# Where six splits of x are issued: in front of the first gate/up pair, or inside it

## The chip, the cores and the metric

The kernel runs on one core of one Trainium2 chip. The metric is device time in microseconds (us): the median of several executions of the same program.

## The reference

One transformer block on x of 2048 rows and 1024 columns, all in float32:

```python
x = x + layernorm(attn(layernorm(x)))       # one head, d = 256, over all 2048 keys
x = x + layernorm(ffn(layernorm(x)))
# attn: qkv = x @ Wqkv + bqkv; softmax(q k^T / 16) v; @ Wo + bo
# ffn:  (silu(x @ W_gate.T) * (x @ W_up.T)) @ W_down.T   with 2752 hidden features
```

## The kernel before

**Precision.** Every float32 operand of a matmul is split in two: `hi`, a cast to fp32r on ScalarE, and `lo`, the rest, by a subtraction on VectorE. A product is then three matmuls, hi·hi, hi·lo and lo·hi. Such pairs of instructions come from `split` (lines 108 and 109) and, where their order is pinned, from `split_later` (lines 406 and 407).

**Attention** runs over 16 blocks of 128 queries. For block i there are `turn` (transposes of the probabilities), `scores` of the next block, `attend` (lines 275 and 276, which read v from the tile `a1` and the transposed probabilities from `a2`), `turn_o` (transposes of the output, line 284, then a split into `oTs`) and `proj` (the matmuls of lines 145 to 147 against `wo_s`, which lies in the tile `wvo`; line 294 adds the bias `bo_s` and scales). `turn_o` and `proj` of block i are issued in step i + 1, those of the last block, NT - 1, after the loop.

**The feed-forward part** works on two halves of 1024 rows. A half has ten pairs of feature blocks (`gate_up`), a rest, and the down projection (`run_down`). A pair is a Strassen-like product of 2 x 2 blocks: seven products, each for gate and for up, each of 12 matmuls (line 604), whose x operands are B11, B21, T2, T1, T3, T4 and B22 in this order. B11 and B21 are parts of x; the T are sums and differences of parts. Four PSUM banks (ag, au, cg, cu; bank 0 to bank 3 in the first half) hold the results. The products with T2 go on accumulating in ag and au, so the first results must be copied out of these banks before: lines 636 and 638. After each group VectorE adds (line 617) and ScalarE applies silu (line 620).

**Where x comes from.** The split operands of the first half lie in `xb` (B11, B21), `kx` (T1, T3), `qa` and `qb` (T2) and `a1` (T4, B22). `a1` is v's tile during attention, and `kx`, `qa`, `qb` hold k and q. The sums of x (line 383) are made during attention and parked in DRAM (`xs_d`). Ten objects of the class `First` bring them back: `load` issues two DMAs (line 428) into a staging tile, `use` splits it into its place (lines 406 and 407). Their list is

```python
order = [t2[0], t13[0], t13[1], t13[2], t2[1], t13[3]] + t4
```

The first four use the staging tiles `f4[2]`, `f4[3]`, `wr[1]` and `xe`, and are split inside the last step of attention. The other six use the same four tiles again; numbers 4 and 5 are the second half of T2 (into `qb`) and the last part of T1/T3 (into `kx`), numbers 6 to 9 are T4 and B22 (into `a1`).

**What sets the order.** A scheduler of the language orders the instructions of each engine by a timeline of its own, from the order of the trace and the dependencies; pinned instructions keep their order in the program among themselves. All these loads and stores go through SP's queue: among them the attention outputs `at_d` (line 296), gate/up weights (line 510, into `f4[4]`, `f2p` and `wr[0]`) and down-projection weights (line 728, into `f4[0:2]`). The weights are split by `Pair.prep` into slots of `a2` and `wvo` as these come free.

**Background jobs.** `gate_up` calls `background()` at three places, which pops one job each. In the first half the jobs of pair p are `ahead(p)` (transposes and loads of late rows, line 346 and 957/958, and sums of down weights, line 733) and `behind(p)` (loads of down weights, the residual of a late row, lines 301 to 307). The staging tiles `wr[1]` and `bo_s` later go to a ring, `raws2`, for the second half and the end.

Of the kernel before, what the change touches and what calls it, by code (L numbers as in the profile page):

```python
# [34 lines left out]
def block_kernel(ctx, tc, x, wqk, wv, bqk, bv, wo, bo, wgu, wlast, wd, out):  # L35
# [17 lines left out]
    def tl(p, shape, dt, name):  # L53
        return p.tile(shape, dt, tag=name, name=name, bufs=1)
# [7 lines left out]
    bo_s = tl(cpool, [P, C], F32, "bo_s")  # L62
# [30 lines left out]
    f4 = [tl(cpool, [P, C], F32, f"f4_{i}") for i in range(5)]  # L93
# [187 lines left out]
    def turn_o(i):  # L281
        b = bank[5][:, 0:D]
        for d in range(2):
            nc.tensor.transpose(b[:, d * P : (d + 1) * P], o_s[i % 2][:, d * P : (d + 1) * P], ident)
        split(oTs[i % 2][:, :, 0, :], oTs[i % 2][:, :, 1, :], b.rearrange("p (d q) -> p d q", d=2))

    def proj(i):
        a = pair[i % 3][0] if i < EARLY else f4[i % 2]
        oT = oTs[i % 2]
        for h, b in ((1, bank[5]), (0, bank[7])):  # L290
            cols = slice(h * 512, h * 512 + 512)
            for d in range(2):
                mm3(b, (oT[:, d, 0, :], oT[:, d, 1, :]), (wo_s[:, d, 0, cols], wo_s[:, d, 1, cols]), d == 0, d == 1)
            nc.vector.scalar_tensor_tensor(a[:, cols], b, ys[i % 4][:, 13:14], bo_s[:, cols], ALU.mult, ALU.add)
        if i >= EARLY:
            nc.sync.dma_start(at_d[i], a)
# [23 lines left out]
    wr = [tl(wpool, [P, C], F32, f"wr{i}") for i in range(2)]  # L320
# [20 lines left out]
    def xpose(t, a, b, banks):  # L341
        for hf in range(2):
            o = banks[hf]
            for j in range(4):
                cb = 4 * hf + j
                nc.tensor.transpose(o[:, j * P : (j + 1) * P], a[:, cb * P : (cb + 1) * P], ident)  # L346
            s = b[:, hf * 512 : hf * 512 + 512]
            nc.scalar.copy(s, o)  # L348
            d = xT_d[t // TB][hf * 512 : hf * 512 + 512, (t % TB) * P : (t % TB + 1) * P]
            nc.sync.dma_start(d.rearrange("(j p) t -> p j t", p=P), s.rearrange("p (j t) -> p j t", j=4))  # L350
# [18 lines left out]
    def xq(name, cb):  # L369
        if name == "T2":  # L370
            return q2[cb // 2][:, cb % 2, :, :]
        t, c = XQ[name]
        return t[:, c + cb, :, :]
# [79 lines left out]
    raws2 = Ring([])  # L453
# [33 lines left out]
    def w4(t):  # L487
        return t.rearrange("p (c h f) -> p c h f", h=2, f=P)
# [112 lines left out]
    def mmc(o, w, m, first, last, chained, pin=lambda m: m):  # L601

        for n, (i, j) in enumerate(((0, 0), (0, 1), (1, 0))):
            one = nc.tensor.matmul(o, w[i], m[j], start=first and n == 0, stop=last and n == 2, skip_group_check=chained)  # L604
            if n == 0:
                pin(one)

    def prod(o, w, a, b, first=True):

        slot, c0 = w.at[a]  # L610
        v = w4(slot.need())
        for cb in range(4):
            x = xq(b, cb)
            mmc(o, (v[:, c0 + cb, 0, :], v[:, c0 + cb, 1, :]), (x[:, 0, :], x[:, 1, :]), first and cb == 0, cb == 3, not first)

    def add(o, a, b, op=ALU.add):
        nc.vector.tensor_tensor(o, a, b, op)  # L617

    def silu(o, a):
        nc.scalar.activation(o, a, AF.Silu)  # L620

    def gate_up(s, p, wg, wu, bg, jobs):

        ag, au, cg, cu = bg
        g11, g12, g22, g21, u11, u12, u22 = tmp[0:7]
        job = list(jobs)

        def background():
            if job:
                job.pop(0)()  # L630

        def put(name, t):
            nc.sync.dma_start(hd[s][p][name], t)

        prod(ag, wg, "A11", "B11")
        nc.scalar.copy(g11, ag)
        prod(au, wu, "A11", "B11")
        nc.scalar.copy(u11, au)
        prod(cg, wg, "A12", "B21")
        wg.slot[0].done()  # L640
        add(g11, cg, g11)
        silu(g11, g11)
        prod(cu, wu, "A12", "B21")
        wu.slot[0].done()
        add(u11, cu, u11)
        add(g11, g11, u11, ALU.mult)
        put("A11", g11)
        background()
        prod(ag, wg, "S2", "T2", False)
        nc.scalar.copy(g12, ag)  # L650
        prod(au, wu, "S2", "T2", False)
        nc.scalar.copy(u12, au)
        prod(cg, wg, "S1", "T1")
        wg.slot[1].done()
        prod(cu, wu, "S1", "T1")
        wu.slot[1].done()
        background()
        prod(ag, wg, "S3", "T3", False)
        nc.scalar.copy(g22, ag)
        add(g22, cg, g22)  # L660
        silu(g22, g22)
        prod(au, wu, "S3", "T3", False)
        nc.scalar.copy(u22, au)  # L663
        add(u22, cu, u22)
        add(g22, g22, u22, ALU.mult)
        put("A22", g22)
        background()
        prod(ag, wg, "A22", "T4", False)
        wg.slot[3].done()
        silu(g21, ag)  # L670
        prod(au, wu, "A22", "T4", False)
        wu.slot[3].done()
        add(g21, au, g21, ALU.mult)
        put("A12", g21)
        prod(cg, wg, "S4", "B22", False)
        wg.slot[2].done()
        add(g12, cg, g12)
        silu(g12, g12)
        prod(cu, wu, "S4", "B22", False)
        wu.slot[2].done()  # L680
        add(u12, cu, u12)
        add(g12, g12, u12, ALU.mult)
        add(u22, g12, g22)
        add(u12, g11, g12, ALU.subtract)
        add(u11, u22, g11, ALU.subtract)
        add(g12, g21, u11, ALU.subtract)
        put("S1", u22)
        put("S3", u12)
        put("S2", u11)
        put("S4", g12)  # L690
# [35 lines left out]
    def load_down(p):  # L726
        for r, fb in zip(f4[0:2], (p, p + NPAIR)):
            nc.sync.dma_start(r, wd[fb * P : (fb + 1) * P, :])

    def down_weights(p):  # L730

        r1, r2 = f4[0:2]
        pin(nc.vector.tensor_tensor(r2[:, R], r2[:, R], r1[:, R], ALU.subtract))
        add(r1[:, R], r1[:, R], r1[:, L], ALU.subtract)
        add(r1[:, L], r2[:, R], r1[:, L])
        add(r2[:, L], r2[:, L], r1[:, L], ALU.subtract)
        for n, t in (("T1", r1[:, R]), ("T3", r2[:, R]), ("T2", r1[:, L]), ("T4", r2[:, L])):
            nc.sync.dma_start(td[p][n], t)
# [145 lines left out]
    for i in range(NT):  # L884
# [35 lines left out]
        if i == NT - 2:  # L920
# [3 lines left out]
            order = [t2[0], t13[0], t13[1], t13[2], t2[1], t13[3]] + t4  # L924
            spare = f4[2], f4[3], wr[1], xe
            for f, r in zip(order, spare):
                f.load(r)
    for n in range(4, 6):
        order[n].load(spare[n % 4])
        order[n].use()  # L930
    turn_o(NT - 1)
    proj(NT - 1)
    for n in range(6, 10):
        order[n].load(spare[n % 4])
        order[n].use()
    spool.release()
    xipool = pool("xi")
    xi = [tl(xipool, [P, C], F32, f"xi{i}") for i in range(4)]
    y = f4[0:4] + xi
    tmp = [xi[i // 2][:, (i % 2) * 512 : (i % 2) * 512 + 512] for i in range(8)]  # L940
    raws2.free(wr[1])
    raws2.free(bo_s)
    for n in range(2, 4):
        slots.free(flat(a2[:, 2 * n : 2 * n + 2, :, :]))
    for n in range(2):
# [3 lines left out]
    def late(p):  # L949
        return EARLY + p if 0 <= p < NT - EARLY else None  # L950

    def ahead(p):

        if late(p - 1):
            xpose(late(p - 1), *f4[2:4], Y[0:2])
        if late(p):
            nc.sync.dma_start(f4[2], at_d[late(p)])
            nc.sync.dma_start(f4[3], x[late(p) * P : (late(p) + 1) * P, :])
        down_weights(p)

    def behind(p):
        if p + 1 < NPAIR:
            load_down(p + 1)
        if late(p):
            residual(late(p), *f4[2:4])

    load_down(0)
    for s in range(2):
        pairs, rest, dn = half[s]
        bg, other = (X, Y) if s == 0 else (Y, X)  # L970
        for p in range(NPAIR):
            jobs = [] if s else [lambda: ahead(p), lambda: behind(p)]
            gate_up(s, p, *pairs[p], bg, jobs)
        gate_up_rest(s, *rest, bg)

        def next_x(cb):
            r1, r2 = raws2.get(), raws2.get()
            build_x(2, cb, r1, r2)
            raws2.free(r1)
            raws2.free(r2)  # L980

        if s == 0:
            run_down(s, dn, other, bg, 2 * TB * [None], [lambda cb=cb: next_x(cb) for cb in range(4)])
        else:
            xpool.release()
            x1pool = pool("x1", side="right")
            x1 = [tl(x1pool, [P, C], F32, f"x1_{k}") for k in range(2 * TB)]
            run_down(s, dn, other, bg, x1, [lambda k=k: nc.sync.dma_start(x1[k], x1_d[2 * TB + k]) for k in range(2 * TB)])
# [39 lines left out]
```

## Time and profile before

| | |
|---|---|
| median of 3 runs | 1729.71 us (1728.43 to 1729.87) |
| the profiled execution's own time | 1728.61 us |
| its span in the trace | 1726.8 us |
| mean granted TensorE clock | 0.992 |
| TensorE busy (PE) | 1699.3 us, 98% of the span |
| VectorE busy (DVE) | 1091.8 us, 63% |
| ScalarE busy (ACT) | 689.1 us, 40% |
| GpSimd busy (POOL) | 89.0 us, 5% |
| moved by DMA | 271.01 MB, mean 157 GB/s |

PE is TensorE's matmuls and PEld its weight loads, which lie beside them. A line such as L604 is a line of the kernel's source; helpers such as `split` put all their instructions on one line, so the tile names tell them apart (buffer numbers are left out: `a` stands for `a1` and `a2`, `f` for `f4` and `f2`, `bank` for all eight). Times within the trace are from the start of the span. The hand-over from attention to the first pair lies near 440 to 460 us.

### The profile page before, as it was taken

To read this page: it belongs to the slowest core of one execution; us is meant where nothing else is said; L and a number is where in the kernel's file an instruction comes from. 1 tells how busy PE (TensorE), PEld (TensorE's weight loads), DVE (VectorE), ACT (ScalarE), POOL (GpSimd) and SP (SyncE) were. 2 spreads that over 40 slices of the span, in tenths; PEclk is the share of its full clock that TensorE was granted. 3 is DMA by queue.
4 is the path that set the end of the run, shared out by engine and by line. 5 is a ranking of instruction groups with operands and counts; after the bars stand their busy time and mean duration, and the time that the engine had idled before them with its cause. 6 is when DMAs were issued, how large, how long until landed. Compare 5 with 4: busy or idle time off the path is not lost.

```text
span 1726.8 us, 21119 instructions
## 1 busy us (share of the span) xinstructions
PE 1699.3 (98%) x7788; PEld 1393.6 (81%) x7788; DVE 1091.8 (63%) x1666; ACT 689.1 (40%) x1031; POOL 89.0 (5%) x118
## 2 busy tenths in 40 slices
PE   8999999999899999999999999999999999999997
PEld 7888887888688888888888888788888888888886
DVE  8633667667877777676378457866555564345458
ACT  3222445544544444443355444433333333244343
POOL 1000001000011111110000000100000000000001
PEclk8999999999899999999999999999999999999999
DMA  6221023234755566665358655633332223486654
GB/s 210 80 80 37 37 74 125 97 126 172 257 195 195 201 215 214 214 204 190 122 191 255 194 194 193 205 105 113 129 109 94 91 92 122 132 280 195 195 185 159
DMA packets 131015, 271.01 MB, mean 157 GB/s; under 512 B 13280, under 2 KB 29792, under 8 KB 130912
## 3 DMA queue, kind: packets, MB, share of 16 engines
q1 hardware_dynamic: 128176, 262.72, 45.6%
q10 hardware_dynamic: 2736, 6.95, 1.1%
q8 instruction: 61, 1.00, 0.2%
q14 instruction: 42, 0.34, 0.1%
HBM read 185.73 MB, written 83.89 MB: 156 GB/s over the span
## 4 chain that ended last, share of the span: by engine, by line
PE 93%; DVE 3%; DMA 2%; issue 1%; ACT 1%; POOL 0%; SPq 0%; POOLq 0%; DVEq 0%; ACTq 0%
PE bank L604 70%; PE bank L146 4%; PE bank L145 4%; PE bank L147 4%; PE bank L275 3%; PE bank L276 2%; PE bank L267 1%; PE bank L205 1%; PE bank L206 1%; PE bank L346 1%; DMA f<-x 1%; PE bank L138 1%; DVE small L115 0%; PE bank L773 0%; PE bank L774 0%
## 5 line engine op out<-in xcount | busy, mean ns | idle before, releaser
L604 PE MATMUL bank<-a 128*128 128x512 f32 x1176 | 273.8, 390 | 0.0
L604 PEld LDWEIGHTS bank<-a 128*128 128x128 f32 x1176 | 220.8, 188 | 46.8
L604 PE MATMUL bank<-xb,a 128*128 128x512 f32 x816 | 197.3, 395 | 0.0
L109 DVE TENSOR_TENSOR a<-f2p,a 128x1024 fp32r<-128x1024 f32 (+2 forms) x114 | 124.7, 1095 | 93.4 <-ACT a L108 81.0
L617 DVE TENSOR_TENSOR xi<-bank,xi 128x512 f32<-128x512 f32 (+1 forms) x168 | 113.3, 685 | 111.1 <-PE bank L604 70.1
L604 PEld LDWEIGHTS bank<-xb,a 128*128 128x128 f32 x816 | 152.9, 187 | 37.1
L604 PE MATMUL bank<-kx,a 128*128 128x512 f32 x648 | 157.1, 395 | 0.0
L604 PE MATMUL bank<-a,a 128*128 128x512 f32 x648 | 153.4, 390 | 0.0
L108 ACT CAST a<-f2p 128x1024 fp32r<-128x1024 f32 (+2 forms) x114 | 107.6, 949 | 112.5 <-PE bank L604 102.4
L109 DVE TENSOR_TENSOR a<-f,a 128x512 fp32r<-128x512 f32 (+3 forms) x93 | 91.3, 981 | 91.4 <-ACT a L108 88.0
L604 PEld LDWEIGHTS bank<-kx,a 128*128 128x128 f32 x648 | 121.5, 187 | 29.5
L604 PEld LDWEIGHTS bank<-a,a 128*128 128x128 f32 x648 | 121.6, 188 | 26.4
L604 PE MATMUL bank<-wvo 128*128 128x512 f32 x600 | 142.4, 390 | 0.0
L604 PEld LDWEIGHTS bank<-wvo 128*128 128x128 f32 x600 | 112.6, 188 | 24.4
L108 ACT CAST a<-f 128x512 fp32r<-128x512 f32 (+3 forms) x93 | 69.4, 747 | 125.7 <-PE bank L604 90.6
L275 PE MATMUL bank<-a,a 128*128 128x512 f32 x256 | 94.5, 402 | 2.8 <-ACT f L348 2.0
L109 DVE TENSOR_TENSOR wvo<-f2p,wvo 128x1024 fp32r<-128x1024 f32 (+2 forms) x48 | 54.8, 1141 | 66.2 <-ACT wvo L108 57.6
L604 PE MATMUL bank<-a,wvo 128*128 128x512 f32 x384 | 93.7, 396 | 1.2 <-ACT xi L663 1.2
L604 PE MATMUL bank<-kx,wvo 128*128 128x512 f32 x384 | 91.9, 390 | 0.0
L617 DVE TENSOR_TENSOR xi<-xi,xi 128x512 f32<-128x512 f32 x124 | 85.4, 688 | 4.3
L604 PEld LDWEIGHTS bank<-a,wvo 128*128 128x128 f32 x384 | 72.0, 188 | 18.8 <-ACT xi L663 1.6
L604 PEld LDWEIGHTS bank<-kx,wvo 128*128 128x128 f32 x384 | 72.1, 188 | 15.7
(234 smaller groups left out, 2751.2 us busy)
## 6 DMA issues: line engine op xcount, KB each, us to landing
f2p<-wgu SPq DMA_DIRECT2D x43, 512.0 KB, 5.0
hd_S<-xi SPq DMA_DIRECT2D x80, 256.0 KB, 4.6
f<-x SPq DMA_DIRECT2D x30, 512.0 KB, 3.9
hd_A<-xi SPq DMA_DIRECT2D x60, 256.0 KB, 2.0
f<-wgu SPq DMA_DIRECT2D x21, 512.0 KB, 4.4
wr<-wgu SPq DMA_DIRECT2D x20, 512.0 KB, 5.9
f<-wd SPq DMA_DIRECT2D x20, 512.0 KB, 5.0
td_T<-f SPq DMA_DIRECT2D x40, 256.0 KB, 4.5
```

The source lines that it names most:

```text
L108: nc.scalar.copy(hi, src)
L109: (lo_engine or nc.vector).tensor_tensor(lo, src, f32(hi), ALU.subtract)
L138: nc.tensor.transpose(b[:, j * P : (j + 1) * P], t[:, cb * P : (cb + 1) * P], ident)
L145: nc.tensor.matmul(o, w[0], m[0], start=first, stop=False)
L146: nc.tensor.matmul(o, w[0], m[1], start=False, stop=False)
L147: nc.tensor.matmul(o, w[1], m[0], start=False, stop=last)
L205: nc.tensor.matmul(b, xg[:, c, 0, cols], wv_s[:, c, :, :].rearrange("p a f -> p (a f)"), start=(c == 0), stop=False)
L206: nc.tensor.matmul(b[:, D:], xg[:, c, 1, cols], wv_s[:, c, 0, :], start=False, stop=(c == 7))
L275: nc.tensor.matmul(b, p[:, k, 0, :], vt[:, k, :, :].rearrange("p h d -> p (h d)"), start=(k == 0), stop=False)
L276: nc.tensor.matmul(b[:, D:], p[:, k, 1, :], vt[:, k, 0, :], start=False, stop=(k == NKB - 1))
L604: one = nc.tensor.matmul(o, w[i], m[j], start=first and n == 0, stop=last and n == 2, skip_group_check=chained)
L617: nc.vector.tensor_tensor(o, a, b, op)
```

## The change

Six of the ten `First` objects are used elsewhere. The loads of numbers 4 to 7 are traced after the last `proj`, with `bo_s` (the bias tile, done with by then) in the place of `xe`. Numbers 4 and 5 are split in a new job `first`, which runs in pair 0 after the copy of u11 (line 638), at a new, fourth `background()` place; this job also issues the loads of numbers 8 and 9. In the other pairs `first` is empty, and `ahead` and `behind` keep their places. Numbers 6 to 9 are split at the head of `ahead(0)`, after the first group's result is stored. `wr[1]` and `bo_s` go to `raws2` there.

```diff
@@ gate_up
         prod(au, wu, "A11", "B11")
         nc.scalar.copy(u11, au)
+        background()
         prod(cg, wg, "A12", "B21")
@@ after the attention loop
-    for n in range(4, 6):
-        order[n].load(spare[n % 4])
-        order[n].use()
     turn_o(NT - 1)
     proj(NT - 1)
-    for n in range(6, 10):
-        order[n].load(spare[n % 4])
-        order[n].use()
+
+    last = f4[2], f4[3], wr[1], bo_s
+    for n in range(4, 8):
+        order[n].load(last[n % 4])
     spool.release()
...
-    raws2.free(wr[1])
-    raws2.free(bo_s)
...
+    def first(p):
+        if p == 0:
+            for n in range(4, 6):
+                order[n].use()
+                order[n + 4].load(last[n % 4])
+
     def ahead(p):
 
+        if p == 0:
+            for n in range(6, 10):
+                order[n].use()
+            raws2.free(wr[1])
+            raws2.free(bo_s)
         if late(p - 1):
...
-            jobs = [] if s else [lambda: ahead(p), lambda: behind(p)]
+            jobs = [] if s else [lambda: first(p), lambda: ahead(p), lambda: behind(p)]
```

## The prediction

> **What bounds the kernel now.** I read the page first: engine totals, then the chain that ended last.
>
> ```profile
> PE 1699.3 (98%) x7788; PEld 1393.6 (81%) x7788; DVE 1091.8 (63%) x1666; ACT 689.1 (40%) x1031; POOL 89.0 (5%) x118
> ...
> PE 93%; DVE 3%; DMA 2%; issue 1%; ACT 1%; POOL 0%; SPq 0%; POOLq 0%; DVEq 0%; ACTq 0%
> ```
>
> TensorE is busy for 98% of the span and is 93% of the chain. Work moved between other engines is worth only the time in which TensorE stands still or is slowed. So I looked for TensorE's holes. At the hand-over from attention to the first pair, TensorE's timeline (start, length, engine, line, operands; in brackets the idle time before and who ended it) has:
>
> ```profile
> 441.79 0.39 PE L147 MATMUL bank<-wvo,oTs 128*128 128x512 f32 x1
> 442.44 0.44 PE L284 MATMUL bank<-ident,f 128*128 128x128 f32 x2 [0.26 <-DVE f L279]
> 443.82 0.50 PE L145 MATMUL bank<-wvo,oTs 128*128 128x512 f32 x1 [0.94 <-ACT oTs L108]
> ...
> 446.31 0.80 PE L145 MATMUL bank<-wvo,oTs 128*128 128x512 f32 x1 [1.76 <-DVE oTs L109]
> ...
> 450.31 0.63 PE L147 MATMUL bank<-wvo,oTs 128*128 128x512 f32 x1
> 454.29 2.93 PE L604 MATMUL bank<-qa,a 128*128 128x512 f32 x6 [3.35 <-ACT xi L636]
> ```
>
> Idle: 0.26 + 0.94 + 1.76 + 3.35 = 6.3 us. The same stretch in windows (busy time of PE, PEld, DVE, ACT, POOL, then granted clock):
>
> ```profile
> 444.00:445.00 1.00, 0.55 (x2) 0.12 (x2) 1.00 (x3) 1.00 (x2) 0.00 (x0) 1.00 0.99 397
> 446.00:447.00 1.00, 0.69 (x2) 0.60 (x3) 1.00 (x3) 0.17 (x1) 0.00 (x0) 0.50 0.77 184
> 458.00:459.00 1.00, 1.00 (x4) 0.81 (x3) 1.00 (x2) 0.00 (x0) 0.00 (x0) 0.50 0.01 4
> ```
>
> The clock falls to half inside the hole and is back only near 459. Ten projection matmuls from 446.31 take 4.4 us, at 0.43 each; a full-speed one takes 0.23 (24 L604 in 5.60 us, 462.17 to 467.77). Loss 2.1. The first 12 products, 454.29 to 459.38, take 5.1 for 2.8: loss 2.3. The hole costs 6.3 + 2.1 + 2.3 = 10.7 us. Why it lasts, ScalarE shows:
>
> ```profile
> 441.50 1.05 ACT L406 CAST qb<-f 128x1024 fp32r<-128x1024 f32 x1
> 442.45 1.05 ACT L406 CAST kx<-f 128x1024 fp32r<-128x1024 f32 x1
> 443.39 0.37 ACT L108 CAST oTs<-bank 128x256 fp32r<-128x256 f32 x1
> ...
> 452.71 1.04 ACT L406 CAST a<-f 128x1024 fp32r<-128x1024 f32 x1 [0.49 <-DMA f<-xT_d]
> 453.66 0.58 ACT L636 COPY xi<-bank 128x512 f32<-128x512 f32 x1
> ```
>
> The copy of the first product (L636) frees bank 0 for T2's product, and stands behind the last split of T4. The chain of waits in this window says what that split waited for:
>
> ```profile
> 446.74 5.89 DMA f<-xT_d
> ...
> 453.75 0.49 ACT xi L636
> ```
>
> [...]
>
> **The change part by part.** Nothing is added or removed in number: the six late splits (two T2/T3, four T4) stay six casts L406 and six subtractions L407, with 12 loads L428. The built program of the changed kernel gives the new order on each engine; times come from the trace. Repeat distances when back to back: ScalarE 0.95 for a 1024-wide cast, 0.5 for a 512-wide; VectorE 1.14 and 0.60, L294 0.66.
>
> 1. The cast of T4's first block now precedes the 512-wide cast of 440.71. Its loads left at 436.27 and 436.64; similar ones land in 3.2 and 3.5, so 440.2. It ends its turn at 441.15: the output transposes start at 442.85, not 442.44. Bounds: 0 to +1.3 (landing 439.5 to 441.5); I take +0.4.
> 2. The oTs cast is no longer behind qb and kx: ready at about 443.6, nearly as now. Its subtraction on VectorE loses the L407s of 442.96 and 444.69, two times 1.14: it runs at 443.95, not 445.83. The ten projection matmuls start at 444.35, not 446.31, and at 0.23 end at 446.75.
> 3. On ScalarE there then stand the 1024-wide cast into wvo, which waits for projection's reads (446.2), a 512-wide cast, and L636: 446.2 + 0.95 + 0.5 + 0.5 = 448.2. The first T2 product starts at 448.2, not 454.29: **-6.1 us**.
> 4. Clock. Holes are now about 0.9, 0.5, 0.3 and 1.4 us with work between them[...]. I take full speed: another **-2.3**; the 12th product ends at 451.0 against 459.38, so **-8.4**. The trace has no half-busy stretch like it, so both ends are kept: 0 or +2.7 (two slow projections, 0.4, and 12 slow products, 2.3).
> 5. Who waits for the moved splits, done against needed. qb cast 449.6 against 450.0; kx cast 450.6 against 453.6; their subtractions 453.9 and 455.0 against 456.2 and 458.3. T4's subtractions: first two 456.8 and 457.9 against 465.0 and 465.7; last two 464.2 and 465.9 against 466.4 and 469.4. Behind the casts ScalarE queues the table load (1.28) and silu, then the bank copies of T2's products, needed at 459.3. Zero cost: TensorE turns to qa, kx products meanwhile. If that cover goes, each us late is a us.
> 6. SP's queue. The two loads into bo_s replace those into xe and go after projection's last add: 448.0 and 448.8, not 437.4; at the slowest landing seen here for such a load (5.9), 454.7, used by a cast at about that time. The last four leave when qb and kx are split: 454.3 to 455.5, not 444.2 to 446.7, landing by 461.4; their casts have their turn at 460.9 and 461.9. at_d, wgu and wd transfers pass ahead. Zero, up to +1 with a 7 us landing.
> 7. Afterwards. VectorE does six L407s (6.8 us) later relative to TensorE, so its lead shrinks. In before, pair 1's L636 ended at 490.05 for a product at 496.3: 6.2 us spare. With my order it ends near 486.4 for 486.9: 0.5 spare. Next, pair 1's u11 copy (L638) stands behind a weight cast released by TensorE itself, 0.95, and the copy of the transposed row, 0.5, so TensorE waits: **+1.0**; plus 0.2 for the thin margin. Bounds 0 to +3.
>
> From pair 2 on the order is the old one and TensorE was without holes, so nothing returns. Sum: -8.4 + 1.0 + 0.2 = **-7.2 us**. Against the profiled execution (1728.61, span 1726.8) that is 1721.4; that execution is 1.1 below the median, 1729.71, so the median forecast is 1722.5.
>
> **The rivals.**
> - Half clock stays. Against it: no hole over 1.5 us. For it: the windows show the drop with some work inside. -7.2 + 2.7 = -4.5: 1725.2.
> - VectorE becomes the bound in pairs 0 and 1. For it: busy 0.96 and 0.94 of the windows 450 to 460 and 470 to 480, and a spare of 0.5. If it is 3.5 us later than worked out, -3.7: 1726.0.
> - Slower: T4's last loads. They leave about 9 us later, wait for two splits, and hold ScalarE's in-order queue, behind which stands the bank 0 copy for T4's product (needed at 464.8). Past about 462, each us goes to TensorE. The gain is gone at 469; it's 0.2% slower from 473, 18 us after issue. The slowest landing listed in this stretch is 7.2 (f<-x), against it. Price at 475: +5.8, 1735.5.
> - The change doesn't do what it says, because the scheduler puts the splits back: 1729.7. The built order speaks against it: qb's and kx's casts follow both bank copies.
>
> **How the numbers follow.** Main case 0.62 (1720.9 to 1725.2 by the bounds of steps 1 and 7), half clock 0.20, VectorE late 0.12, late loads 0.05, no effect 0.01. A measurement tells 0.2%, 3.5 us, from no change. Faster: 0.62 + most of half clock, 0.15, + a little of the third, 0.03 = 0.80. Same 0.15. Slower 0.05. Range 1720.0 to 1726.5: from just below the main case's lower end, since steps are rounded to tenths, to just past the VectorE case.
>
> **What would show it.** Right: L604 on qa starting near 448, with the hole under 3.5 us in all, 0.23 per matmul in it, oTs' subtraction before 444.5, L636 ahead of qb's cast; a TensorE wait of about 1 us on L638 near 493. Wrong: granted clock 0.5 after 446 (first rival); PE waiting for L407, L617 or L636 of pair 1 for several us (second); PE idle until a cast after a landing past 462 (third).

## The result and the profile after

| | median us | against the kernel before, same chip |
|---|---|---|
| before | 1728.41 (1726.91 to 1729.87, 14 runs) | |
| changed | 1725.49 (1722.46 to 1729.04, 14 runs) | 0.9981 [0.9974, 0.9989] |

By this ratio the changed kernel is faster by 0.19%, 3.3 us [1.9, 4.5]; the two medians are 2.9 apart. The forecast was a gain of 7.2 (from 1729.71 to 1722.5), so less than half of it came. The profiled execution of the changed kernel took 1725.89, its span is 1724.1.

The page of the changed kernel: engine totals (busy us, share, instructions) and the shares of the chain that ended last:

```profile
PE 1696.0 (98%) x7788; PEld 1391.4 (81%) x7788; DVE 1091.7 (63%) x1666; ACT 689.0 (40%) x1031; POOL 87.0 (5%) x118
...
PE 94%; DMA 2%; DVE 2%; issue 1%; ACT 1%; POOL 0%; SPq 0%; POOLq 0%; DVEq 0%; ACTq 0%
```

The counts are the same. TensorE's busy time fell by 3.3 us and the span by 2.7, so TensorE stood idle for 28.1 us, against 27.5 before. Over the whole kernel its holes did not get smaller: those that closed at the hand-over came back elsewhere, and what is left of the gain is matmuls that no longer ran at half clock. The hand-over in TensorE's timeline of the changed kernel (start, length, engine, line, operands; in brackets the idle time before and who ended it):

```profile
443.51 0.44 PE L284 MATMUL bank<-ident,f 128*128 128x128 f32 x2 [0.62 <-DVE f L279]
444.41 0.50 PE L145 MATMUL bank<-wvo,oTs 128*128 128x512 f32 x1 [0.46 <-ACT oTs L108]
...
449.13 2.13 PE L604 MATMUL bank<-qa,a 128*128 128x512 f32 x8 [1.44 <-ACT xi L636]
...
468.97 5.77 PE L604 MATMUL bank<-a,a 128*128 128x512 f32 x24 [2.96 <-ACT xi L660]
...
492.95 1.66 PE L604 MATMUL bank<-qa,a 128*128 128x512 f32 x6 [1.42 <-ACT xi L636]
...
500.67 1.66 PE L604 MATMUL bank<-qa,a 128*128 128x512 f32 x6 [1.00 <-ACT xi L638]
```

The holes of the hand-over are 0.62, 0.46 and 1.44 instead of 6.3 us together (2.5). Below them stand three waits that the kernel before did not have: 2.96 ahead of the products with T4 in pair 0, and 1.42 and 1.00 ahead of pair 1's T2 products. The same 20 us in windows (busy time of PE, PEld, DVE, ACT, POOL, then granted clock), first the kernel before, then the changed one:

```profile
440.00:460.00 20.00, 13.69 (x40) 9.65 (x40) 17.12 (x22) 12.41 (x17) 0.00 (x0) 0.66 0.67 231
```

```profile
440.00:460.00 20.00, 17.48 (x76) 13.22 (x76) 15.81 (x22) 12.01 (x17) 0.00 (x0) 1.00 0.64 215
```

76 matmuls instead of 40, at a granted clock of 1.00 instead of 0.66.

Executions start attention a little differently, so I count from the last attention matmul (L276, at 440.51 before and 441.22 after). The first qa product starts 13.78 after it before the change and 7.91 after it in the changed kernel; the 12th product ends at +18.87 and +10.8: 8.1 us gained. Of these, 3.8 are idle time and 4.3 the clock. The three new waits take back 5.4. Net 2.7; a wait of 1.43 near 1120 us (L604 for L620 and L663) that the profile of before shows and this one does not adds to it, and the whole stretch to the last matmul is 1276.56 against 1272.69, 3.9 shorter. That wait near 1120 comes and goes between executions (0.87 in a second profile of the changed kernel), so I don't count it as the change's.

### The profile page after: what moved, and what is told of

The parts are those of the page before. It is cut to its first block, busy times and chain, and to the rows that moved or that the text cites. A ratio compares the mean times of both kernels' runs of the same rounds, so it can differ in the third digit from the quotient of the medians.

```text
span 1724.1 us, 21116 instructions
## 1 busy us (share of the span) xinstructions
PE 1696.0 (98%) x7788; PEld 1391.4 (81%) x7788; DVE 1091.7 (63%) x1666; ACT 689.0 (40%) x1031; POOL 87.0 (5%) x118
## 3 DMA queue, kind: packets, MB, share of 16 engines
q10 hardware_dynamic: 2736, 6.95, 1.2%
## 4 chain that ended last, share of the span: by engine, by line
PE 94%; DMA 2%; DVE 2%; issue 1%; ACT 1%; POOL 0%; SPq 0%; POOLq 0%; DVEq 0%; ACTq 0%
PE bank L604 71%; PE bank L146 4%; PE bank L145 4%; PE bank L147 4%; PE bank L275 3%; PE bank L276 2%; PE bank L205 2%; PE bank L267 1%; PE bank L206 1%; PE bank L138 1%; DMA f<-x 1%; PE bank L346 1%; DMA f<-xT_d 0%; PE bank L774 0%; PE bank L775 0%
## 5 line engine op out<-in xcount | busy, mean ns | idle before, releaser
L604 PE MATMUL bank<-a 128*128 128x512 f32 x1176 | 273.7, 390 | 0.0
L604 PEld LDWEIGHTS bank<-a 128*128 128x128 f32 x1176 | 220.8, 188 | 46.8
L604 PE MATMUL bank<-xb,a 128*128 128x512 f32 x816 | 197.3, 395 | 0.0
L604 PEld LDWEIGHTS bank<-xb,a 128*128 128x128 f32 x816 | 152.9, 187 | 37.1
L617 DVE TENSOR_TENSOR xi<-bank,xi 128x512 f32<-128x512 f32 (+1 forms) x168 | 113.2, 685 | 108.5 <-PE bank L604 67.3
L604 PE MATMUL bank<-kx,a 128*128 128x512 f32 x648 | 157.4, 395 | 0.0
L604 PE MATMUL bank<-a,a 128*128 128x512 f32 x648 | 153.7, 390 | 3.0 <-ACT xi L660 3.0
L604 PEld LDWEIGHTS bank<-a,a 128*128 128x128 f32 x648 | 121.6, 188 | 29.7 <-ACT xi L660 3.4
L604 PEld LDWEIGHTS bank<-kx,a 128*128 128x128 f32 x648 | 121.5, 187 | 29.4
L604 PE MATMUL bank<-wvo 128*128 128x512 f32 x600 | 142.4, 390 | 0.0
L604 PEld LDWEIGHTS bank<-wvo 128*128 128x128 f32 x600 | 112.6, 188 | 24.3
L604 PE MATMUL bank<-a,wvo 128*128 128x512 f32 x384 | 93.7, 395 | 0.0
L604 PE MATMUL bank<-kx,wvo 128*128 128x512 f32 x384 | 91.9, 390 | 0.0
L617 DVE TENSOR_TENSOR xi<-xi,xi 128x512 f32<-128x512 f32 x124 | 85.3, 688 | 4.2
L604 PEld LDWEIGHTS bank<-a,wvo 128*128 128x128 f32 x384 | 72.1, 188 | 17.2
L604 PEld LDWEIGHTS bank<-kx,wvo 128*128 128x128 f32 x384 | 72.1, 188 | 15.7
```

## What made the last loads late

ScalarE's timeline of the changed kernel shows who held the copy L660, for which TensorE waited 2.96:

```profile
466.07 1.04 ACT L406 CAST a<-f 128x1024 fp32r<-128x1024 f32 x1 [3.94 <-DMA f<-xT_d]
467.39 1.04 ACT L406 CAST a<-f 128x1024 fp32r<-128x1024 f32 x1 [0.28 <-DMA f<-xT_d]
468.34 0.58 ACT L660 COPY xi<-bank 128x512 f32<-128x512 f32 x1
```

The last two splits, numbers 8 and 9, wait 3.94 us for their loads and the copy stands behind them. SP's queue in the same kernel shows when these loads left:

```profile
450.10 0.38 SPq L296 DMA_DIRECT2D at_d<-f  x1
...
451.05 0.66 SPq L510 DMA_DIRECT2D f<-wgu  x1
457.02 0.33 SPq L729 DMA_DIRECT2D f<-wd  x1
...
457.93 0.38 SPq L428 DMA_DIRECT2D f<-xs_d  x1
...
459.31 0.69 SPq L428 DMA_DIRECT2D f<-xT_d  x1
```

Between 451.05 and 457.02 SP issued nothing, although the subtractions of qb and kx, for which these loads wait, ended at 454.8 and 455.9. At the head of its queue stood the load of down weights into `f4[1]`, and `f4[1]` was still the source of at_d's last store (line 296 stores from `f4[i % 2]`), issued at 450.10 and landing 6.9 later, at 457.0. The list of DMA issues gives the landing:

```profile
at_d<-f SPq DMA_DIRECT2D x1, 512.0 KB, 6.9
...
f<-xs_d SPq DMA_DIRECT2D x2, 256.0 KB, 7.6
f<-xT_d SPq DMA_DIRECT2D x2, 256.0 KB, 7.8
```

The kernel before has the same wait in its queue: the store left at 453.53 and landed 5.0 later, and the load of down weights left at 458.58, with nothing issued between them. There no load of T4 stood behind it.

## What made pair 1 late

VectorE and GpSimd of the changed kernel, one line each:

```profile
488.53 3.15 DVE L109 TENSOR_TENSOR wvo<-f2p,wvo 128x1024 fp32r<-128x1024 f32 x1 [0.19 <-ACT wvo L108]
```

```profile
487.64 2.95 POOL L303 TENSOR_TENSOR f<-f,f 128x1024 f32<-128x1024 f32 x1 [2.65 <-DMA f<-wd]
```

A 1024-wide subtraction, 1.22 elsewhere and 1.13 from one to the next back to back, took 3.15. GpSimd's residual addition of a late row ends at 490.59, the subtraction 1.09 after that. Behind it on VectorE stands L617 (491.60), which L636 waits for, and TensorE waits for L636 until 492.95. In the trace of before a 512-wide one beside such an addition (L303, 478.82 to 481.52) took 2.29 instead of 0.69 and ended 0.55 after it:

```profile
479.78 2.29 DVE L109 TENSOR_TENSOR a<-f,a 128x512 fp32r<-128x512 f32 x1
```

Both times most of a full duration, 1.09 of 1.22 and 0.55 of 0.69, lies behind the end of the addition, as if the subtraction had waited for it. That is read from these times alone; what the two engines contend for is not shown.

The third wait, 1.00 on L638, is another matter. That copy stands on ScalarE behind a cast of 1.05 which TensorE itself releases (498.60) and the copy of the transposed row (L348), and runs at 500.03, as step 7 of the prediction has it.

## The experiments

Theory: the hand-over gained what the prediction says, and two things took most of the difference back: the last loads, late by SP's queue, and lateness in pair 1, made by the six moved subtractions, this collision and ScalarE's order ahead of L638. The rivals are in the expectations. "Stretch" is from the last L276 to the last matmul in the profile (before 1276.56, changed 1272.69), and holds the wait near 1120 too: 1.43 before, 0 changed, 0.87 in ctl_after, 0.72 in a_own_staging, 0.3 or less in the others. Each ratio is to the kernel before on the same chip.

| run | median us | ratio | stretch |
|---|---|---|---|
| ctl_after | 1725.55 | 0.9982 [0.9975, 0.9988] | 1272.48 |
| a_own_staging | 1723.88 | 0.9972 [0.9961, 0.9984] | 1269.65 |
| s_shift_rows | 1722.06 | 0.9962 [0.9949, 0.9974] | 1269.29 |
| as_both | 1721.29 | 0.9955 [0.9942, 0.9967] | 1268.00 |
| d_t4_only | 1724.85 | 0.9982 [0.9975, 0.9989] | 1272.51 |
| e_t23_only | 1726.41 | 0.9987 [0.9979, 0.9996] | 1273.79 |
| w_before_fill | 1726.32 | 0.9989 [0.9982, 0.9995] | 1273.25 |
| best_late9 | 1719.20 | 0.9949 [0.9935, 0.9962] | 1267.28 |
| bs_before_shift | 1727.56 | 0.9995 [0.9986, 1.0003] | 1275.36 |
| b_res_vector | 1722.46 | 0.9962 [0.9950, 0.9975] | 1269.28 |
| q_wd_behind | 1719.49 | 0.9954 [0.9937, 0.9971] | 1266.70 |
| qs_wd_shift | 1718.84 | 0.9940 [0.9926, 0.9954] | 1266.97 |

**The changed kernel again (ctl_after).** No edit.

> The changed kernel again, beside the others on the same chip. Both theories (late loads, VectorE's backlog) expect its profile to repeat: TensorE at full clock through the hand-over, first T2 product about 8 us earlier after the last attend matmul than before would have it by its 12th product, then waits of about 3.0 us (T4's bank copy L660), 1.4 us (L636 in pair 1) and 1.0 us (L638 in pair 1). Time 2 to 4 us under the kernel before.

The waits are there again: 1.63 before the products with T4, 1.42 and 1.00 in pair 1. The last two are the same in both profiles; the first differs, and the casts ahead of L660 wait for loads that landed sooner here (6.3 and 6.6 us after issue, not 7.6 and 7.8).

**Every late load with a staging tile of its own (a_own_staging).** On the changed kernel; the six loads no longer wait for a split.

```diff
-    last = f4[2], f4[3], wr[1], bo_s
-    for n in range(4, 8):
-        order[n].load(last[n % 4])
...
+    for n, r in zip(range(4, 10), (f4[2], f4[3], wr[1], xi[3], xi[1], bo_s)):
+        order[n].load(r)
...
-                order[n + 4].load(last[n % 4])
```

> The changed kernel with staging tiles of their own for T4's last three loads (xi[3], xi[1] and bo_s), so that the last two no longer wait for the splits of qb and kx to free f4[2] and f4[3]. Late loads: the wait of 3.0 us on L660 in pair 0 goes (0 to 0.5 left) and the time falls by 2.5 to 3.0 us against the changed kernel. VectorE's backlog: L660's wait goes too, but TensorE then reaches pair 1 earlier than VectorE is ready, the waits on L636 and L638 grow from 2.4 to 4 or 5 us, and the time falls by 0.5 us or less.

The wait on L660 is gone and the stretch is 2.8 shorter than the second profile of the changed kernel, where that wait was 1.63. Pair 1's waits did not grow to take it back. In TensorE's timeline they are one, of 1.63 on the transposes of a late row:

```profile
489.32 1.09 PE L346 MATMUL bank<-ident,f 128*128 128x128 f32 x8 [1.63 <-ACT f L307]
```

So L660's wait can go without coming back in pair 1. Its price alone is not shown: the scheduler also placed the late row's addition on GpSimd earlier (476.50), where it meets no subtraction of `wvo` (1.17 here), and L638 no longer waits. Nor does this run tell why the loads were late, since it changes staging and queue together.

**The late rows one pair later (s_shift_rows).** On the changed kernel: pair 0 has no late row, so pair 1's beginning has no residual on GpSimd and fewer jobs on VectorE.

```diff
     def late(p):
-        return EARLY + p if 0 <= p < NT - EARLY else None
+        return EARLY + p - 1 if 1 <= p <= NT - EARLY else None
```

> The changed kernel with the late rows of x (loads, residual, transposes) one pair later, pairs 1 to 8 in place of 0 to 7; the output is the same. It takes off VectorE in pair 0 four bn_stats (2.4 us) with what goes with them, and the GpSimd addition beside which one VectorE split took 3.15 us in place of 1.22; it leaves T4's loads as they are. VectorE's backlog: the two waits in pair 1 (1.4 and 1.0 us) go, the L660 wait of 3.0 stays: 2.4 us faster than the changed kernel. Late loads: if the two waits in pair 1 only follow from pair 0's lateness they stay at about 2 us, and the time falls by under 0.7 us.

TensorE's waits after the hand-over:

```profile
467.97 5.74 PE L604 MATMUL bank<-a,a 128*128 128x512 f32 x24 [1.79 <-ACT xi L660]
...
496.41 1.66 PE L604 MATMUL bank<-qa,a 128*128 128x512 f32 x6 [0.32 <-ACT xi L638]
```

Pair 1's 2.4 us became 0.3; L660's wait stayed. The two losses are separate. The stretch is 3.2 shorter than in ctl_after, 0.9 of it near 1120.

**The same shift on the kernel before (bs_before_shift).**

> The kernel before with only the late rows one pair later (pairs 1 to 8), nothing else. In its profile TensorE has no wait in pairs 0 and 1 after the hand-over, so VectorE's lead is worth nothing there: the backlog theory expects no change (within 0.7 us of before) and the hand-over's hole as it was, 6.3 us idle and half clock. If the late rows' work itself slows the kernel (GpSimd's addition, the transposes, the DMAs beside the hole), this kernel is 2 us or more faster, and the gain of the kernels with both edits is partly not the change's.

Ratio 0.9995 [0.9986, 1.0003]: no difference that can be told, and at most 2.4 us, where the changed kernel is 3.5 us faster with the shift than without (0.9962 and 0.9982). So the shift mostly repairs a loss that the change made. The hand-over here is not quite as it was: the clock came back at 448.85, during the projection, which ended sooner, the last hole became 4.72 instead of 3.35, and the first T2 product started 14.41 after the last L276 instead of 13.78.

**The residual on VectorE (b_res_vector).** On the changed kernel, the late row of pair 0 alone:

```diff
-        (nc.gpsimd if t >= EARLY else nc.vector).tensor_tensor(xt, xt, a, ALU.add)
+        (nc.gpsimd if t > EARLY else nc.vector).tensor_tensor(xt, xt, a, ALU.add)
```

> The changed kernel with the residual addition of the first late row (row block 8, in pair 0) on VectorE in place of GpSimd. Collision: in the changed kernel the wvo split took 3.15 us on VectorE while GpSimd's addition ran (487.6 to 490.6), and L636 of pair 1 waited behind it for 1.4 us. Without the collision the split takes 1.2 us again; VectorE takes over an addition of about 1.2 us, which by its place in the order may come before or behind; the L636 wait falls to 0 to 0.7 us and the time by 0.7 to 1.4 us. VectorE's work alone: the added 1.2 us of VectorE offsets it, the wait of pair 1 stays at 1 us or more, and the time is the same.

VectorE now does the addition too, and is still done sooner:

```profile
485.75 1.22 DVE L303 TENSOR_TENSOR f<-f,f 128x1024 f32<-128x1024 f32 x1
486.88 1.22 DVE L109 TENSOR_TENSOR wvo<-f2p,wvo 128x1024 fp32r<-128x1024 f32 x1
```

Addition and subtraction together take 2.4, less than the 3.15 that the subtraction alone took beside GpSimd. L636's wait is 0.35: the collision, not the amount of work, made 1.1 of its 1.42. L638's wait is gone for another reason. In this kernel that copy stands ahead of the cast behind which the changed kernel has it:

```profile
495.31 0.59 ACT L638 COPY xi<-bank 128x512 f32<-128x512 f32 x1 [1.57 <-DMA hd_S<-xi]
495.80 1.05 ACT L108 CAST a<-f 128x1024 fp32r<-128x1024 f32 x1
```

That is one reason why the kernel gains more than the 0.7 to 1.4 expected of the collision: 1722.46, 3.5 us below the changed kernel by the ratios. L660's wait is 1.50.

**Both repairs (as_both), and number 9 split later (best_late9).** as_both joins the edits of a_own_staging and s_shift_rows; best_late9 moves one split on top of it:

```diff
         if p == 0:
-            for n in range(6, 10):
+            for n in range(6, 9):
                 order[n].use()
...
     def behind(p):
+        if p == 0:
+            order[9].use()
+            raws2.free(bo_s)
```

> Both edits on the changed kernel: own staging tiles for T4's last loads, and the late rows one pair later. If the shortfall of the changed kernel against the forecast is made of the L660 wait and the two waits in pair 1 and nothing else, all three go and the time is about 5 us below the changed kernel, 8 us below the kernel before. If VectorE's backlog from the six moved subtractions (6.8 us) is the bound by itself, 2 us or more of waits stay in pair 1.

> Both edits (own staging, late rows one pair later) and, besides, the last T4 block (number 9, staged in bo_s) is split one background job later, so that the first bank copy of T2's products (L651) no longer stands behind a cast that waits for bo_s's load; it waited 1.3 us there. Late loads: that wait goes to 0 to 0.3, and with it the kernel is 1.0 to 1.3 us below the one with both edits. VectorE's backlog: the wait turns up in pair 1 and the time is the same as with both edits.

as_both keeps one wait, a cast that stood for its load (into `bo_s`) ahead of L651:

```profile
462.31 5.74 PE L604 MATMUL bank<-kx,wvo 128*128 128x512 f32 x24 [1.26 <-ACT xi L651]
```

With number 9 behind L651 there is no wait after the hand-over until 510 us, and the stretch is 9.3 us shorter than before, 1.1 of it near 1120: the whole hand-over gain is kept.

**Each half of the change alone (d_t4_only, e_t23_only).** In d numbers 4 and 5 are split in front as before and 6 to 9 inside the pair; in e only 4 and 5 are inside.

```diff
@@ d_t4_only, on the changed kernel
+    for n in range(4, 6):
+        order[n].load(spare[n % 4])
+        order[n].use()
     turn_o(NT - 1)
...
-    for n in range(4, 8):
+    for n in range(6, 10):
         order[n].load(last[n % 4])
...
-            for n in range(4, 6):
-                order[n].use()
-                order[n + 4].load(last[n % 4])
+            pass
@@ e_t23_only, on the changed kernel
-    last = f4[2], f4[3], wr[1], bo_s
-    for n in range(4, 8):
-        order[n].load(last[n % 4])
+    stage = f4[2], f4[3], wr[1], xe, p_s[:, 0:C], p_s[:, C:T]
+    for n in range(4, 10):
+        order[n].load(stage[n - 4])
+        if n > 5:
+            order[n].use()
...
-                order[n + 4].load(last[n % 4])
...
-            for n in range(6, 10):
-                order[n].use()
```

> Half of the change: only T4's four splits (numbers 6 to 9) are inside pair 0; numbers 4 and 5 are split in front of the last proj, as in the kernel before. ScalarE and VectorE then again do qb's and kx's halves ahead of oTs. Forecast's steps 2 to 4: oTs' subtraction returns to about 446 and the 1.8 us hole in front of proj is back; L636 has no T4 cast in front of it, so the last hole is 1 to 2 us instead of 3.4; whether the clock falls decides 2.5 us. Sum about 2 to 4 us of the 8 us gained at the hand-over. If instead T4's late landing alone made the hole (the rest being hidden anyway), this kernel gains as much at the hand-over as the whole change.

> The other half: only numbers 4 and 5 are split inside pair 0; T4's four splits stay in front of L636, with staging of their own (wr[1], xe and the two halves of p_s), so their loads need not wait for qb and kx. Steps 2 to 4: oTs is early and the hole in front of proj is gone (about 1.8 us), but four casts (3.8 us) and their landings stand in front of L636: a last hole of 3 us or more, and half clock after it. Gain at the hand-over 1 to 3 us. If the two holes in front of proj were all that mattered, it would be 6 us or more.

The first T2 product of each, d first:

```profile
453.03 2.93 PE L604 MATMUL bank<-qa,a 128*128 128x512 f32 x6 [1.62 <-ACT xi L636]
```

```profile
453.60 2.93 PE L604 MATMUL bank<-qa,a 128*128 128x512 f32 x6 [6.00 <-ACT xi L636]
```

In d the ten projection matmuls and about seven products run at half clock (0.43 to 0.45 from one to the next, not 0.23); in e the projection is early and at full clock, the hole before T2 is 6.00 long, and about fourteen products run at half clock. Counted to the end of the first 48 products the gain at the hand-over is 2.2 in d, 1.1 in e and 8.1 in the changed kernel: the halves do not add up, since each leaves a hole in which the clock fell, at 445.86 in d (1.75 long) and at 449.51 in e (6.00). d has no later wait, and so equals the whole change (0.9982 and 0.9981).

**The hole filled with work that nobody needs (w_before_fill).** On the kernel before, 40 transposes into a free bank after the last projection, whose last matmul is pinned so that they follow it. Lines stand two later: L606 is the product L604 and L638 the copy L636.

```diff
+    for _ in range(40):
+        tc.keep_in_program_order(nc.tensor.transpose(bank[4][:, 0:P], ident, ident))
     for n in range(6, 10):
```

> The kernel before, with 40 dummy transposes of the identity into an idle bank between the last projection matmul and T2's first product, in the hole in which TensorE waits for L636. No other engine's order changes. Clock theory (a hole with half clock costs more than its idle time): the clock is full again by the first product, the 12 products take 2.8 us in place of 5.1, L636 still ends at the same place, and the kernel is 2.3 us faster than the one before. Rival (the first products are slow for another reason[...]): the same time, or up to 1 us slower for dummies that run past the end of the hole.

```profile
449.86 5.07 PE L936 MATMUL bank<-ident 128*128 128x128 f32 x40
455.22 1.66 PE L606 MATMUL bank<-qa,a 128*128 128x512 f32 x6 [0.29 <-ACT xi L638]
```

T2's product still starts late, at 455.22 (0.85 later than before, counted from the last L276, since the last cast of T4 waited 1.37 for its load and not 0.49), but six matmuls take 1.66 instead of 2.93, and all twelve 2.88 instead of 5.09: 2.2 for the clock, where step 4 put 2.3. The ratio, 0.9989 [0.9982, 0.9995], is 1.9 us [0.9, 3.1]. The clock was at half from 447.54 to 450.95, TensorE was busy for all of these 3.41 us, and it came back under the transposes.

**Down weights behind the last loads (q_wd_behind).** On the changed kernel: the loads of numbers 8 and 9 and then pair 0's down-weight loads are pinned in this order, so that the latter stand behind; the splits of 8 and 9 are traced in `behind(0)`, and the copies L651 and L653 of pair 0 are pinned ahead of them. In this kernel the late row's loads reach `f4[2]` and `f4[3]` before those two splits, so B22 and a part of T4 are made of other data; the work is the same in kind and number.

```diff
-                nc.sync.dma_start(r[:, h], d)
+                m = nc.sync.dma_start(r[:, h], d)
+                if self in order[8:]:
+                    pin(m)
...
                 order[n + 4].load(last[n % 4])
+            load_down(0)
...
-            nc.sync.dma_start(r, wd[fb * P : (fb + 1) * P, :])
+            d = nc.sync.dma_start(r, wd[fb * P : (fb + 1) * P, :])
+            if p == 0:
+                pin(d)
```

> In the changed kernel the last four loads (L428 into f4[2], f4[3]) stand on SP's queue behind the load of down weights into f4[1], which stood from 451.05 to 457.02 because at_d's last store out of f4[1] had not landed. Here the two loads of down weights are put behind these four loads, so nothing stands ahead of them but the gate/up loads. The splits keep their places as far as the scheduler allows; it puts the copy of the product with T3 (L660 of the changed kernel) ahead of the cast from f4[2] and that of L664 between the two casts, so this wait alone doesn't tell the theories apart: issue and landing do. Theory (the queue made the loads late): they leave right after the subtractions of qb and kx, 454.9 to 456.5 instead of 457.9 to 459.3, about 3 us earlier, land by 463 to 464 instead of 466 to 467, and TensorE's wait before a1's products, 2.96, falls to 0.5 or less; the down weights come later by 3 to 6 us, which costs nothing if they are not needed soon; median 1722 to 1724. Rival (the DMA engines were the limit, not the queue): the four leave earlier, but land at 466 to 467 all the same, 10 us after issue; the wait stays 1.5 to 3, median as the changed kernel's, 1725 to 1726.

The last four loads left from 453.83 to 455.33 and took 4.2 and 5.0 us by the list of DMA issues, so they were there by about 460.5. TensorE had no wait after the hand-over. But the casts stood elsewhere on ScalarE and waited for the late row, so this run shows the loads' times and not yet what they are worth. Its median is 2.5 us below the 1722 to 1724 expected, and pair 1 has no wait either: more went than L660's wait.

**The same with the late rows one pair later (qs_wd_shift).** Here numbers 8 and 9 find their own data, and casts and copies stand on ScalarE as in s_shift_rows.

> The run before (q_wd_behind) and the shift of the late rows by one pair (s_shift_rows) together: no late row is loaded in pair 0, so numbers 8 and 9 find their own data in f4[2] and f4[3]. On ScalarE the casts from f4[2] and f4[3], and the copies L660 and L664 behind them, stand here as in s_shift_rows; on SP's queue the two loads of down weights stand behind the last four loads. Theory (SP's queue makes the loads late): the four leave at 454 to 455.5 and land in 4 to 5 us, as in q_wd_behind, by 461; both casts have their turn at once and TensorE's wait of 1.79 before a1's products in s_shift_rows goes to 0 to 0.3, the stretch from the last L276 to the last matmul is 1267 to 1268, the median 1719 to 1720.5. Rival (the order of ScalarE made the wait go in q_wd_behind, since there the copy stood ahead of the cast): the wait stays at 1.2 to 1.8, the stretch at 1269, the median at 1721.5 to 1722.5.

SP's queue, then ScalarE, in their timelines (lines of this source stand a little later: L430 is the load L428, L734 the down-weight load L729, L665 the copy L660):

```profile
454.03 0.33 SPq L430 DMA_DIRECT2D f<-xs_d  x1
...
455.54 0.42 SPq L430 DMA_DIRECT2D f<-xT_d  x1
456.01 0.90 SPq L734 DMA_DIRECT2D f<-wd  x2
```

```profile
461.21 2.00 ACT L406 CAST a<-f 128x1024 fp32r<-128x1024 f32 x2
463.11 0.58 ACT L665 COPY xi<-bank 128x512 f32<-128x512 f32 x1
```

Counted from the last L276 the loads left 3.0 to 3.1 us earlier than in the changed kernel (3.8 to 3.9 on the trace's own time), landing after 4.9 and 5.2 instead of 7.6 and 7.8, both casts without a wait. L660's wait of 1.79 in s_shift_rows is gone, and nothing replaced it. The stretch is 2.3 shorter than in s_shift_rows. This settles the queue: the loads were late because they stood behind a load that waited for a store, and behind its transfer; the two go together here and are not told apart. It has also the lowest median of all, 1718.84, 0.60% [0.46, 0.74] below the kernel before; best_late9's interval overlaps with it, so the two are not told apart.

## Why the prediction was right, and where it fell short

- **Steps 1 to 3, right.** The attention of the profiled changed kernel ends 0.71 later than that of before; with this the forecast start of the first T2 product, 448.2, is 448.9, and it was 449.13. The hole of 1.76 in front of the projection is gone, and that of 0.94 became 0.46.
- **Step 4, right.** The granted clock was 1.00 through the whole hand-over. The least busy 3.41 us in the changed kernel (446.0 to 449.4, for one) have 1.98. w_before_fill shows how near the edge is: there 3.41 us with 1.66 busy ended at half clock. It also gave the clock's share its own measurement.
- **Hand-over in all:** 8.1 measured, 8.4 forecast.
- **Step 5, right:** TensorE had no wait on qb, kx or T4's first splits.
- **Step 6, wrong.** "Zero, up to +1 with a 7 us landing" became +2.96 (1.63 in the second profile). The forecast let the last four loads leave when their tiles were split, 454.3 to 455.5. I had the order of SP's queue but did not ask what each entry ahead of them waits for; the down-weight load ahead waits for at_d's landing. The landing of 7.4 to 8.0 us instead of at most 5.9 came on top. It is the third rival's mechanism at a price of 3, not 13. The two loads into `bo_s` missed too: forecast to be there by 454.7, they let their cast start at 457.75 (6.1 and 7.1 from issue to landing), but TensorE did not wait for that one.
- **Step 7, half right.** L638's +1.0 came as priced, 1.00, and by the order that the step names. "Plus 0.2 for the thin margin" was 1.42: the spare of 0.5 was worked out with VectorE at its own speed, and the collision with L303 costs 1.9. The collision could be read in the profile of before: there L303 (478.82, 2.70 long) met the 512-wide subtraction of 479.78, which took 2.29 instead of 0.69, where nothing waited for it.
- **The sum.** -8.1 + 5.4 = -2.7 in place of -7.2; with the 1.4 near 1120 that were absent it is -4.1, against -3.9 in the stretch. The first two rivals were not it: the clock held, and VectorE was late by one collision in pair 1, not bound through two pairs.
- **The number.** That 1725.49 fell in the range is in part luck. It lies above the main case (1720.9 to 1725.2); the range reached it only to take in the first two rivals, at 1725.2 and 1726.0, which did not happen. What did happen was the late loads, which had been given 0.05, and a collision that had no price.

What stays open is why the wait near 1120 us comes and goes between executions of one kernel.

## What to carry to other kernels

When a transfer is moved within a queue like SP's here, ask of every entry ahead of it what that entry waits for, stores whose tile it overwrites above all: behind a held-up one the last loads left 3.0 to 3.1 us later than ahead of it. When a change eats slack, look in the old trace for durations that are already stretched beside a neighbour engine (2.29 instead of 0.69 here), since they cost nothing only as long as the slack is there. Moving work out of the hole paid here by the hole and by the clock (3.8 and 4.3 us), and the work's new place should be tried with its loads and its neighbours moved as well: here that turned 0.19% into 0.60%.

## What the hardware showed that I had not expected

- Moving an addition from GpSimd to VectorE made VectorE earlier: 2.4 us for two operations in a row, 3.15 for one of them beside GpSimd's.
- The clock changed in steps of 3.41 us: at the hand-over every stretch at half clock lasted a whole multiple of it. By the granted clock in windows of 0.1 us, five of these kernels lost it. The table has the times, in us, and in brackets how long TensorE was busy in the 3.41 us that ended there.

  | run | lost at | back at | at half clock |
  |---|---|---|---|
  | before | 445.49 (1.27) | 459.14 (3.41) | 13.65 |
  | bs_before_shift | 445.44 (1.17) | 448.85 (2.91) | 3.41 |
  | the same, again | 452.27 (0.99) | 459.09 (3.41) | 6.82 |
  | d_t4_only | 445.86 (1.17) | 456.10 (3.07) | 10.24 |
  | e_t23_only | 449.51 (1.50) | 459.75 (3.41) | 10.24 |
  | w_before_fill | 447.54 (1.66) | 450.95 (3.41) | 3.41 |

  The last column is 4, 1, 2, 3, 3 and 1 times 3.41. Cut into such blocks from these times on and back, the blocks near the hand-over that kept the full clock were busy for 2.22 or more, those that lost it for 0.99 to 1.66, those that did not bring it back for 2.74 or less, and those that did for 2.91 or more. None that lost it was idle throughout. Where the blocks begin differs between executions: the kernel before and w_before_fill do the same work up to the projection, with the same holes (0.26, 0.94, then 1.76 and 1.75), and lost the clock 4.98 and 6.95 after the last L276. So with the same holes all ten projection matmuls ran at half clock in the one, five to six of them in the other. The changed kernel and six of the eight runs that keep all of it have a mean granted clock of 1.00 from 440 to 460; for the other two, ctl_after and best_late9, the mean over the whole run is 0.996 and 0.997, as high as in those six (0.995 to 0.996). In the changed kernel no 3.41 us there have less than 1.98.
- The four last loads, 256 KB each, took 7.4 to 8.0 us to land in the changed kernel, behind the held-up load of down weights, and 4.9 and 5.2 (medians of two each) in qs_wd_shift, ahead of it.
